# A graph network's attention sums: edges sorted within and across partitions, and bf16 one-hot products in place of f32 ones

## The chip, the cores and the metric

The kernel runs on one core of one Trainium2 chip. The metric is the device time of one execution in microseconds. The time before is the median of three runs. The profile is of one further execution, and all lengths inside the kernel come from it.

## The reference, cut to what matters

The input is 6250 nodes of 256 values and two edge lists. Four layers follow each other, each added to x: a graph convolution over 106,250 edges with 256 attributes each, an expert layer whose gates come from graph attention over 131,072 other edges, a second graph convolution, and a second expert layer. The change concerns the attention (`x` is the normalised node matrix, `M` the number of nodes):

```python
h = (x_flat @ W_gat).reshape(M, HEADS, NUM_EXPERTS)          # 4 heads, 4 experts
a_src = (h * att_src).sum(-1); a_dst = (h * att_dst).sum(-1)
e = leaky_relu(a_src[src] + a_dst[dst], 0.2)
ee = exp(e - segment_max(e, dst)[dst])
denom = segment_sum(ee, dst)
msg = h[src] * (ee / (denom[dst] + 1e-16))[:, :, None]
agg = segment_sum(msg, dst) + b_gat       # then a norm, a mean over heads, the two best experts
```

Indices reach up to 8191 while there are 6250 nodes, and a source beyond the end counts as the last node: 23,793 edges come from the last node, 76,190 from the others, and the rest, whose destination lies outside, is dropped. The sum over edges with the same destination is what both versions do with matrix products.

## The kernel before, in words

Nodes lie in 49 blocks of 128, one node a partition. Three stages follow a short start.

**First layer** (to about 1263 us). A loop over 147 steps `q` (L1600) loads edge attributes, turns them on VectorE (`turn`, L1465), multiplies them in f32 (`hidden`, L1473, tile `ph`), adds gathered rows (`join`, L1483) and sums by destination (`add_up`, L1490, tile `pe`). The order of every engine is written by hand and pinned. In between, `steps(sort)` takes one or two steps of `sorting()` (L1582): the attention's edges are sorted here, ahead of their use. Each of the 128 partitions holds 1024 edges as one key each (`make_keys`, L1244: destination reversed, source in the low 13 bits, read as an f32). `sort_steps` (L1276) takes the eight largest of each partition (`V.max`) and strikes them out (`V.match_replace`), 106 times. `sorted_edges` (L1285) then takes the keys apart in one go: `src2` (source), `high` (destination's block), `low` (node in the block), the latter also turned and written to `low_dram`; it ends with 160 small memsets and a count of the edges that lie in their expected blocks.

**Attention and first expert layer** (about 1291 to 2345 us). After the sort a column holds one edge of each partition, and eight columns make a group `g`; there are 80 groups. Since each partition was sorted alone, the 128 edges of a column spread over up to 12 blocks; `near_blocks` (L932) states which. The loop at L2187 works on several groups at once, one round per group:

- `fetch` (L1772): eight indirect DMAs on GpSimd gather the source rows into `sg` (five buffers).
- `score` (L1777): `rb`, the group's `low` values broadcast from `low_dram`, becomes a one-hot tile in bf16 (L1785); products with `part`, the three bf16 parts of `a_dst`, give `pa` (L1789). `A` marks each edge's block.
- `weigh` (L1803): picks the block (`za`), sums (`z`), leaky relu, exp on ScalarE.
- `spread_out` (L1817): the payload, 20 values an edge, goes to a PSUM tile `px` (L1824); `pp` (L1831) is the payload laid out over all blocks of the group, f32; `B` (L1840) is the one-hot of `low`, f32.
- `add_up` (L1845): one f32 product per column, `po` += `B`.T `pp` (L1852), over all blocks at once; then `po` is added to `acc` (L1858).
- `count_last` (L1861): counts the edges from the last node by destination, in the first rounds.

Between these calls stand `slot()` calls (L2166), five in a round up to round 61 and four after it. Each advances the expert layer `experts1` (L1652) by one of its 396 steps (eight f32 records on TensorE; products `ph` with gelu on ScalarE into `hh`, and `py` into `ys`), and takes up the work that follows the gates (`gates`, `node_values`). Each engine works its instructions in order, nearly the order of these calls. A block's gates can start when no later group can add to it (`complete`).

**Second graph convolution and second expert layer** (2345 us to the end). Gathers on GpSimd (`hg`, L1128), one-hot tiles on VectorE and products `pe` on TensorE. It starts when the last node's `hp` is written. The flag `redo` runs a general path if a count says that an edge was missed.

Of the kernel before, what the change touches and what calls it, by code (L numbers as in the profile page):

```python
# [8 lines left out]
F32 = mybir.dt.float32  # L9
# [7 lines left out]
P = 128  # L17
# [10 lines left out]
class Ordered:  # L28
# [6 lines left out]
    def pin(self):  # L35

        new = []
        for i in reversed(self.traced):
            if i is self.at:
                break  # L40
            new.append(i)
        for i in reversed(new):
            if i.engine in self.last:
                self.tc.add_manual_dep(
                    i, self.last[i.engine],
                    mybir.DependencyInfo(
                        mybir.DependencyClass.NoSync, mybir.DependencyReason.DATA
                    ),
                    reason="keep_in_program_order",
                )  # L50
            self.last[i.engine] = i.name
        self.at = self.traced[-1]

# [815 lines left out]
def kernel(ctx: ExitStack, tc: tile.TileContext, a: dict, out: bass.AP):  # L869
# [49 lines left out]


    KA, KB, KT, KM, NK = 640, 544, 848, 596.0, 12
# [3 lines left out]
    assert C2 % 8 == 0 and KA % P == 0 and P % G == 0 and N <= 8192 - P and T >= NK  # L925
# [5 lines left out]

    def near_blocks(g):  # L932

        k = g * G + G / 2
        mid = k * (N / KM) / P
        spread_of = (C2 * (k / C2) * (1 - k / C2)) ** 0.5 * (N / KM) / P
        n = min(NK, int(-(-2 * (4.2 * spread_of + 0.9) // 1)))
        b0 = min(max(round(mid - n / 2), 0), T - 2)
        return b0, min(max(round(mid - n / 2) + n, b0 + 2), T) - b0
# [4 lines left out]
    with ExitStack() as fast:  # L944
# [12 lines left out]
        lane16 = const.tile([P, P], BF16, name="lane16")  # L957
        with tc.tile_pool(name="numbers", bufs=1) as numbers:
# [6 lines left out]
            V.tensor_copy(lane16, jn)  # L965
# [240 lines left out]

        def equal(pool, w, q):


            eq = pool.tile([P, G1 * P], F32, name="eq", bufs=3)  # L1210
# [28 lines left out]
        src2 = gat.tile([P, KA], I32, name="src2")  # L1239
        low = gat.tile([P, KT], BF16, name="low")  # L1240
        high = gat.tile([P, KT], BF16, name="high")
        good3 = gat.tile([P, 2, 2], F32, name="good3")

        def make_keys(ix, k):  # L1244
# [4 lines left out]
            for i in range(2):  # L1249
# [22 lines left out]
                raw[1], raw[1], 13, 0x10000000, op0=OP.logical_shift_left, op1=OP.bitwise_or  # L1272
# [3 lines left out]
        def sort_steps(k):  # L1276

            top = order[:, k * 8 : (k + 1) * 8]
            V.max(out=top, in_=key)
            yield  # L1280
            if k * 8 + 8 < KT:
                V.match_replace(out=key, in_to_replace=top, in_values=key, imm_value=0.0)
            yield

        def sorted_edges(pst, wk):  # L1285

            k = order.bitcast(I32)
            V.tensor_scalar(src2, k[:, 0:KA], 8191, None, op0=OP.bitwise_and)
            some = key[:, 0:KT]
            for v, s in ((high, 20), (low, 13)):  # L1290
# [4 lines left out]
                V.tensor_copy(some, vi)  # L1295
                V.tensor_scalar(some, some, -1.0, 127.0, op0=OP.mult, op1=OP.add)
                V.tensor_copy(v, some)
            for c in range(KA // P):
                pt = pst.tile([P, 4, P], F32, name="pt")
                TE.transpose(pt[:, 0, :], some[:, c * P : (c + 1) * P], ident)  # L1300
                lt = wk.tile([P, P], BF16, name="lt")
                SC.activation(lt, pt[:, 0, :], AF.Copy)
                SC.dma_start(low_dram[c * P : (c + 1) * P, :], lt)
            V.tensor_add(good2[:, 1:2], good3[:, 0, 0:1], good3[:, 1, 0:1])
            V.tensor_add(good2[:, 3:4], good3[:, 0, 1:2], good3[:, 1, 1:2])

            lim = key[:, 0:KA]
            for g in range(KA // G):
                V.memset(lim[:, g * G : (g + 1) * G], float(near_blocks(g)[0]))
            hit = order[:, 0:KA]  # L1310
            V.tensor_tensor(hit, high[:, 0:KA], lim, op=OP.is_ge)
            for g in range(KA // G):
                V.memset(lim[:, g * G : (g + 1) * G], sum(near_blocks(g)) - 0.5)
            V.tensor_tensor(lim, lim, high[:, 0:KA], op=OP.is_ge)
            V.tensor_mul(hit, hit, lim)
            V.tensor_reduce(good2[:, 0:1], hit, axis=AX.X, op=OP.add)
# [5 lines left out]
        with ExitStack() as layer:  # L1322
# [3 lines left out]
            order = srt.tile([P, KT], F32, name="order")  # L1326
# [109 lines left out]
            HS = D + 8  # L1436
            with (
# [144 lines left out]
                def sorting():  # L1582

                    for k in range(KT // 8):
                        yield from sort_steps(k)
                    sorted_edges(psm, wk)
# [49 lines left out]
        acc = sums.tile([P, T, HV], F32, name="acc")  # L1636
# [101 lines left out]
        with (  # L1738
# [6 lines left out]
            tc.tile_pool(name="px3", bufs=1, space=PSUM) as psx,  # L1745
# [9 lines left out]
            px = psx.tile([P, P + 2 * G * HV], F32, name="px")  # L1755
            lanes = px[:, 0:P]
            V.tensor_copy(lanes, lane)
# [3 lines left out]
            NA = KA // G  # L1761
            HG = G // 2
            rows, near, got, pas, zs, pps, Bs, pos = {}, {}, {}, {}, {}, {}, {}, {}
# [8 lines left out]
            def fetch(g):  # L1772
                got[g] = wk.tile([P, G, GW], F32, name="sg", bufs=5)
                for j in range(G):
                    gather(got[g][:, j, :], gat_dram, src2[:, g * G + j : g * G + j + 1])

            def score(g, half):  # L1777

                b0, n = near_blocks(g)
                if half == 0:  # L1780
# [4 lines left out]
                    V.tensor_scalar(rows[g], rows[g], pid, None, op0=OP.is_equal)  # L1785
                    pas[g] = psa.tile([P, G, NK * H], F32, name="pa")
                for j in range(half * HG, (half + 1) * HG):
# [6 lines left out]
                if half == 1:  # L1794
                    rows.pop(g)
                    near[g] = wk.tile([P, G, NK], F32, name="A", bufs=3)
                    V.tensor_tensor(
                        near[g][:, :, 0:n], lanes[:, None, b0 : b0 + n].to_broadcast([P, G, n]),
                        high[:, g * G : (g + 1) * G].unsqueeze(2).to_broadcast([P, G, n]),
# [3 lines left out]
            def weigh(g):  # L1803
                n = near_blocks(g)[1]
                za = wk.tile([P, G, NK, H], F32, name="za", bufs=1)[:, :, 0:n, :]
                V.tensor_mul(
                    za, pas.pop(g)[:, :, 0 : n * H].rearrange("p g (b h) -> p g b h", h=H),
                    near[g][:, :, 0:n].unsqueeze(3).to_broadcast([P, G, n, H]),
                )
                z = wk.tile([P, G, H], F32, name="z")  # L1810
                V.tensor_reduce(z, za.rearrange("p g b h -> p g h b"), axis=AX.X, op=OP.add)
                V.tensor_add(z, z, got[g][:, :, HV:])
# [4 lines left out]
            def spread_out(g, half):  # L1817


                n = near_blocks(g)[1]  # L1820
                at = P + g % 2 * G * HV
                pay = px[:, at : at + G * HV].rearrange("p (g v) -> p g v", v=HV)
                if half == 0:
                    V.tensor_mul(  # L1824
                        pay.rearrange("p g (x h) -> p g x h", h=H),
                        got.pop(g)[:, :, 0:HV].rearrange("p g (x h) -> p g x h", h=H),
                        zs.pop(g).unsqueeze(2).to_broadcast([P, G, X + 1, H]),
                    )
                js = slice(half * HG, (half + 1) * HG)
                pps[g, half] = wk.tile([P, HG, NK, HV], F32, name="pp", bufs=3)  # L1830
                V.tensor_tensor(  # L1831
                    pps[g, half][:, :, 0:n, :],
                    pay[:, js, :].unsqueeze(2).to_broadcast([P, HG, n, HV]),
                    near[g][:, js, 0:n].unsqueeze(3).to_broadcast([P, HG, n, HV]), op=OP.mult,
                )
                if half == 1:
                    near.pop(g)
                Bs[g, half] = wk.tile([P, HG, P], F32, name="B", bufs=3)
                k = g * G + half * HG
                V.tensor_tensor(  # L1840
                    Bs[g, half], lanes[:, None, :].to_broadcast([P, HG, P]),
                    low[:, k : k + HG].unsqueeze(2).to_broadcast([P, HG, P]), op=OP.is_equal,
                )

            def add_up(g, half):  # L1845
                b0, n = near_blocks(g)
                if half == 0:
                    pos[g] = pso.tile([P, NK, HV], F32, name="po")
                po = pos[g][:, 0:n, :]
                B, pp = Bs.pop((g, half)), pps.pop((g, half))  # L1850
                for j in range(HG):
                    TE.matmul(  # L1852
                        po.rearrange("p b v -> p (b v)"), B[:, j, :],
                        pp[:, j, 0:n, :].rearrange("p b v -> p (b v)"),
                        start=half == 0 and j == 0, stop=half == 1 and j == HG - 1,
                    )
                if half == 1:
                    V.tensor_add(acc[:, b0 : b0 + n, :], acc[:, b0 : b0 + n, :], po)  # L1858
                    pos.pop(g)

            def count_last(k):  # L1861

                b = wk.tile([P, G, P], BF16, name="b", bufs=1)
                V.tensor_tensor(
                    b, lanes[:, None, :].to_broadcast([P, G, P]),
                    low[:, k : k + G].unsqueeze(2).to_broadcast([P, G, P]), op=OP.is_equal,
                )
                q = wk.tile([P, G, T], BF16, name="q", bufs=1)
                V.tensor_tensor(
                    q, lane64[:, None, :].to_broadcast([P, G, T]),  # L1870
                    high[:, k : k + G].unsqueeze(2).to_broadcast([P, G, T]), op=OP.is_equal,
                )
                pc = psy.tile([P, 2, D], F32, name="py")[:, 0, :]
                for j in range(G):
# [752 lines left out]
```

## Time and profile before

| | |
|---|---|
| median of 3 runs | 4173.14 us (4166.47 to 4188.83) |
| the profiled execution's own time | 3417.51 us |
| its span, first to last instruction | 3415.6 us |
| TensorE clock granted, mean | 0.905 of full speed |
| busy: TensorE, VectorE, GpSimd, ScalarE | 3169.8, 2303.3, 2243.9, 1127.5 us |
| start; first layer; attention with expert layer; its tail; second half | 150; 1113 (and 28 of passage); 977; 77; 1071 us |

The first two rows differ by 22%: the profiled execution was quicker than the three timed ones. In the views below, a group is written as line, engine, operation, result <- operands, shapes and count, then its busy time and the mean of one in ns, then the idle time of the engine just before it and what ended that. An f32 product shows as two records. In a table of stretches each engine's busy time is followed by its number of instructions.

### The profile page before, as it was taken

The numbers are of one execution on the slowest core, as the hardware profiler recorded it, in microseconds if no ns is written. First come the engines' busy times: TensorE is split into PE (matmuls) and PEld (weight loads), VectorE is DVE, ScalarE is ACT, GpSimd is POOL, SyncE is SP. The second block draws the span as 40 slices with busy tenths as digits, with TensorE's granted clock in tenths as the row PEclk, the third lists the DMA queues.
The fourth block names the chain that finished last, engine by engine and source line by source line (L and its number), as shares of the span: only waits on it lengthen the run. The fifth ranks groups of instructions, "written<-read, shape, count | busy, mean of one in ns | idle before, by whom it ended". The sixth has DMA issues, their size and how long they took to land.

```text
span 3415.6 us, 57212 instructions
## 1 busy us (share of the span) xinstructions
PE 3169.8 (93%) x18509; PEld 2532.5 (74%) x18509; DVE 2303.3 (67%) x5687; ACT 1127.5 (33%) x2014; POOL 2243.9 (66%) x2364
## 2 busy tenths in 40 slices
PE   7899999999999989999999999995688988989998
PEld 5677777777777778888888888883456666666677
DVE  7788898888888867877575858775234444445464
ACT  4122222222222234445545455661012212212134
POOL 0677777677777746766555556625777777777773
PEclk9999999999999999999999999996567677677797
DMA  6899999999999953434343434443112222222221
GB/s 182 197 205 203 203 205 202 194 203 205 205 209 206 207 133 107 98 83 138 83 125 97 132 85 126 114 98 88 53 53 59 60 59 60 59 59 66 59 63 37
DMA packets 699200, 428.56 MB, mean 125 GB/s; under 512 B 531304, under 2 KB 640347, under 8 KB 698892
## 3 DMA queue, kind: packets, MB, share of 16 engines
q0 software_dynamic: 89408, 178.08, 23.1%
q1 hardware_dynamic: 366236, 187.21, 21.2%
q10 hardware_dynamic: 243248, 59.52, 9.9%
q8 instruction: 150, 2.46, 0.3%
q14 instruction: 158, 1.29, 0.1%
HBM read 382.05 MB, written 42.49 MB: 124 GB/s over the span
## 4 chain that ended last, share of the span: by engine, by line
PE 62%; POOL 12%; DMA 10%; issue 7%; DVE 5%; SPq 1%; ACT 1%; ACTq 0%; DVEq 0%; POOLq 0%
PE ph L1115 31%; POOL hg L1128 12%; PE py L1115 11%; PE po L1852 6%; PE pe L1509 5%; DMA hg<-hp_dram,src 5%; PE pt L1115 4%; DMA ea<-in_edge_attr_dram 3%; PE pe L2492 3%; DMA rb<-low_dram 1%; PE pa L1789 1%; PE pt L1109 1%; DVE et L1468 1%; DVE x_all L2033 1%; SPq L1146 0%
## 5 line engine op out<-in xcount | busy, mean ns | idle before, releaser
L1128 POOL DMA_INDIRECT h<-y_dram,src x882 | 840.6, 953 | 414.2 <-issue 261.4
L1128 POOL DMA_INDIRECT hg<-hp_dram,src x831 | 786.0, 946 | 267.9 <-issue 225.5
L1128 POOL DMA_INDIRECT sg<-gat_dram,src x640 | 612.4, 957 | 351.1 <-issue 161.6
L1115 PE MATMUL ph<-w1b,et 128*128 128x256 f32 x3528 | 825.9, 386 | 9.8 <-DVE et L1468 9.8
L1115 PEld LDWEIGHTS ph<-w1b,et 128*128 128x128 f32 x3528 | 657.3, 191 | 152.9 <-issue 70.5
L2492 PE MATMUL pe<-eq,hg 128*128 128x96 f32 (+15 forms) x2036 | 438.1, 352 | 151.1 <-DMA hg<-hp_dram,src 123.4
L2492 PEld LDWEIGHTS pe<-eq,hg 128*128 128x128 f32 x2036 | 385.7, 258 | 256.1 <-issue 94.1
L2471 DVE TENSOR_SCALAR eq<-px,dst,ew 128x96 f32<-128x96 f32 x831 | 262.0, 370 | 219.1 <-PE pe L2492 135.3
L1487 ACT ACTIVATE h<-h 128x1536 f32<-128x1536 f32 x147 | 218.2, 1484 | 552.4 <-DMA ea<-in_edge_attr_dram 206.5
L1115 PE MATMUL py<-w,hh 128*128 128x256 f32 x1568 | 383.8, 385 | 4.8 <-ACT hh L1688 4.3
L1115 PE MATMUL ph<-b_all,w 128*128 128x256 f32 (+1 forms) x1600 | 385.9, 380 | 0.8 <-ACT hh L1688 0.7
L1486 DVE TENSOR_TENSOR h<-ph,h 128x1536 f32<-128x1536 f32 x147 | 258.2, 1757 | 122.5 <-PE ph L1115 118.9
L1115 PEld LDWEIGHTS py<-w,hh 128*128 128x128 f32 x1568 | 289.1, 191 | 40.9 <-ACT hh L1688 6.5
L1115 PEld LDWEIGHTS ph<-b_all,w 128*128 128x128 f32 x1600 | 289.9, 190 | 32.9 <-ACT hh L1688 1.1
L1468 DVE STREAM_TRANSPOSE et<-ea 128x1536 f32<-128x1536 f32 x147 | 259.9, 1768 | 12.6 <-DMA ea<-in_edge_attr_dram 9.2
L1688 ACT ACTIVATE hh<-ph,b 128x256 f32<-128x256 f32 (+1 forms) x400 | 166.5, 467 | 278.9 <-PE ph L1115 277.9
L1852 PE MATMUL po<-pp,B 128*128 128x240 f32 (+10 forms) x1280 | 252.1, 337 | 2.3 <-DVE acc L1858 2.2
L1852 PEld LDWEIGHTS po<-pp,B 128*128 128x128 f32 x1280 | 215.6, 190 | 14.4 <-DVE acc L1858 2.9
L1509 PE MATMUL pe<-h,eq 128*32 128x257 f32 x3168 | 217.9, 385 | 0.0
L1509 PEld LDWEIGHTS pe<-h,eq 128*32 128x32 f32 x3168 | 96.3, 109 | 84.6 <-issue 31.9
L1831 DVE TENSOR_TENSOR pp<-px,A 128x960 f32<-128x960 f32 (+10 forms) x160 | 156.1, 975 | 3.8 <-PE po L1852 3.6
L1688 ACT ACT_TABLE_LOAD x98 | 125.7, 1283 | 53.9 <-PE ph L1115 48.3
(338 smaller groups left out, 3950.2 us busy)
## 6 DMA issues: line engine op xcount, KB each, us to landing
ea<-in_edge_attr_dram ACTq DMA_DIRECT2D x588, 96.0 KB
ea<-in_edge_attr_dram SPq DMA_DIRECT2D x588, 96.0 KB
y<-y SPq DMA_DIRECT2D x196, 128.0 KB
w<-in_L_ffn_W_dram SPq DMA_DIRECT2D x48, 512.0 KB
y<-ys SPq DMA_DIRECT2D x96, 256.0 KB
rb<-low_dram SPq DMA_DIRECT2D x80, 256.0 KB
h<-y_dram,src POOLq DMA_INDIRECT x882
hg<-hp_dram,src POOLq DMA_INDIRECT x831
```

Of the source, the lines that this page charges most:

```text
L1109: TE.transpose(pt[:, c, :], src[:, c * P : (c + 1) * P], ident)
L1115: TE.matmul(dst, lhs(c), rhs(c), start=c == 0, stop=c == n - 1)
L1128: GP.indirect_dma_start(out=dst, out_offset=None, in_=table[0:NP, :], in_offset=IndirectOffsetOnAxis(ap=idx, axis=0),)
L1468: V.transpose(et[q].rearrange("p c m k -> p m c k"), ahead.pop(q).rearrange("p i m (c k) -> p (i m) c k", c=2),)
L1486: V.tensor_add(h, ph.pop(q), h)
L1487: SC.activation(h, h, AF.Relu)
L1509: TE.matmul(sums[w][b * Q : (b + 1) * Q, :], eq[k][:, j, at], h[:, i * NT + j, 0:WS], start=g == 0 and j == NT - 1, stop=g == last_of[b] a ...
L1688: SC.activation(hidden[u][:, f, :n, :], ph[:, f - f0, :n, :], AF.Gelu, bias=b1[:, e, f : f + 1],)
L1831: V.tensor_tensor(pps[g, half][:, :, 0:n, :], pay[:, js, :].unsqueeze(2).to_broadcast([P, HG, n, HV]), near[g][:, js, 0:n].unsqueeze(3).to ...
L1852: TE.matmul(po.rearrange("p b v -> p (b v)"), B[:, j, :], pp[:, j, 0:n, :].rearrange("p b v -> p (b v)"), start=half == 0 and j == 0, stop ...
L2471: V.tensor_scalar(equals[k][:, j, :], lanes[:, 0:NW], dst_of[:, t : t + 1], ew[:, t : t + 1], op0=OP.is_equal, op1=OP.mult,)
L2492: TE.matmul(sums[b][:, lo - t0 * P : hi - t0 * P], hg[:, j, :], eq[:, j, lo - n0 : hi - n0], start=False, stop=after >= (t0 + n) * P,)
```

## The change

The sort becomes two sorting networks of max and min on VectorE. The first sorts each partition's 1024 keys down to runs of eight; TensorE turns the tile so that eight columns of 128 partitions lie in one row (`turn_keys`); the second network sorts those; a second turn puts them back. So a column now holds 128 edges with neighbouring destinations. `sorted_tiles` computes beforehand, from binomial means and deviations, which blocks each tile (column) can meet: one to seven, where the whole group met up to 12. There are 84 groups and 612 tiles. The counts are now a column of ones in the payload.

The payload is weighted in SBUF (`weight`) and split into three bf16 parts, by copies on ScalarE and subtractions on VectorE, 61 columns with the column of ones. `spread_out` makes one tile `E` per column: the one-hot over all nodes of the tile's blocks, in bf16, by one tensor_scalar. `add_up` makes one bf16 product per tile and block. Only `acc` at the end (in `gates`) adds the three parts up. `px`, `pp` and `B` go, `sg` has four buffers, `po` two PSUM banks. The buffers of `y` for even nodes lie in `gtab`. The core of the diff:

```diff
-            top = order[:, k * 8 : (k + 1) * 8]
-            V.max(out=top, in_=key)
-            if k * 8 + 8 < KT:
-                V.match_replace(out=key, in_to_replace=top, in_values=key, imm_value=0.0)
+        def sort_steps(here, there, least):
+            size = 2
+            while size <= C2:
+                step = size // 2
+                while step >= (least if size == C2 else 1):
...
+                    for some, up in runs if size < C2 else [(slice(0, 1), 0)]:
+                        x, y = a[:, some, :, 0, :], a[:, some, :, 1, :]
+                        V.tensor_tensor(b[:, some, :, up, :], x, y, op=OP.max)
+                        V.tensor_tensor(b[:, some, :, 1 - up, :], x, y, op=OP.min)
+                        yield
...
+        def turn_keys(pst, here, there):
+            for k in range(0, G, 4):
+                pt = pst.tile([P, 4, P], F32, name="pt")
+                for i in range(4):
+                    TE.transpose(pt[:, i, :], here[:, :, k + i], ident)
+                SC.activation(there[:, k : k + 4, :], pt, AF.Copy)
+                yield
+        def sort_all(pst):
+            yield from sort_steps(key, order, G)
+            yield from turn_keys(...)
+            yield from sort_steps(order, key, P)
+            yield from turn_keys(...)
...
-            lim = key[:, 0:KA]
-            for g in range(KA // G):
-                V.memset(lim[:, g * G : (g + 1) * G], float(near_blocks(g)[0]))
...
+        block = gat.tile([P, KA], BF16, name="block")
+        GP.memset(block, 0.0)
+        # ... 379 more memsets: each tile's first block
...
-                got[g] = wk.tile([P, G, GW], F32, name="sg", bufs=5)
+                got[g] = wk.tile([P, G, GW], F32, name="sg", bufs=4)
...
-                    pps[g, half][:, :, 0:n, :],
-                    pay[:, js, :].unsqueeze(2).to_broadcast([P, HG, n, HV]),
-                    near[g][:, js, 0:n].unsqueeze(3).to_broadcast([P, HG, n, HV]), op=OP.mult,
-                )
...
-                    Bs[g, half], lanes[:, None, :].to_broadcast([P, HG, P]),
-                    low[:, k : k + HG].unsqueeze(2).to_broadcast([P, HG, P]), op=OP.is_equal,
+            def weight(g, step):
+                m = len(tiles2[g])
+                parts = [pays[g % 2][:, 0:m, i * HV : (i + 1) * HV] for i in range(3)]
+                if step == 0:
+                    pay[g] = wk.tile([P, G, HV], F32, name="pay", bufs=1)[:, 0:m, :]
+                    V.tensor_mul(pay[g]..., got.pop(g)..., zs.pop(g)...)
+                    SC.activation(parts[0], pay[g], AF.Copy)
+                elif step == 1:
+                    V.tensor_sub(pay[g], pay[g], parts[0])
+                    SC.activation(parts[1], pay[g], AF.Copy)
+                else:
+                    V.tensor_sub(parts[2], pay.pop(g), parts[1])
+            def spread_out(g, j):
...
+                Es[g, j] = wk.tile([P, NM, P], BF16, name="E", bufs=EB)
+                V.tensor_scalar(
+                    Es[g, j][:, 0:n, :].rearrange("p b k -> p (b k)"), nodes16[:, 0 : n * P],
+                    bits.bitcast(F32)[:, g * G + j : g * G + j + 1], None, op0=OP.is_equal,
+                )
...
-                    TE.matmul(
-                        po.rearrange("p b v -> p (b v)"), B[:, j, :],
-                        pp[:, j, 0:n, :].rearrange("p b v -> p (b v)"),
+                for b in range(b0, b0 + n):
+                    bank, to = divmod(b - u0, UB)
+                    TE.matmul(
+                        pos[g][:, bank, to * HP : (to + 1) * HP], E[:, b - b0, :],
+                        pays[g % 2][:, j, :], start=bank not in begun,
...
+                def spread_and_sum(i):
+                    for q in (2 * i, 2 * i + 1):
+                        if there in range(NA):
+                            spread_out(there, q)
+                        g, j = divmod(there * G + q - LAG, G)
+                        if g in range(NA):
+                            add_up(g, j)
```

Here `EB` is 6 and `LAG` 4: the product of a tile is issued four tiles after its `E`. In a round the calls stand in the order `weight(there, 1)`, `spread_and_sum(0)`, slot, `score(now, 0)`, slot, `weight(there, 2)`, `spread_and_sum(1)`, `weigh(here)`, slot, `spread_and_sum(2)`, slot, `score(now, 1)`, slot, `weight(here, 0)`, `spread_and_sum(3)`, `count_last`.

## The prediction

> **What bounds the kernel now.** I first cut the span into stages (busy time of each engine in six stretches; TensorE, its weight loads, VectorE, ScalarE, GpSimd, granted clock, DMA share, GB/s).
>
> ```profile
> 150.00:1263.00 1113.00, 1091.34 (x7233) 845.18 (x7232) 948.51 (x1645) 309.93 (x522) 803.84 (x844) 1.00 0.99 201
> 1291.00:2268.00 977.00, 966.34 (x6696) 857.35 (x6695) 706.66 (x1723) 490.11 (x856) 612.40 (x640) 1.00 0.41 108
> 2268.00:2345.00 77.00, 54.29 (x310) 43.70 (x310) 61.20 (x203) 37.91 (x79) 15.44 (x15) 0.85 0.38 113
> 2345.00:3416.00 1071.00, 916.76 (x3604) 677.02 (x3603) 468.10 (x1763) 225.67 (x416) 774.60 (x820) 0.72 0.20 57
> ```
>
> The second row is the attention stage with the expert layers, 80 rounds at 12.2 us. TensorE is busy 99% of it; VectorE has 270 us to spare. The change sits here, and its sort in the first row, also TensorE's. The last row it does not touch. A busy sum can hide waits, so I read next the groups of the attention stage:
>
> ```profile
> L1852 PE MATMUL po<-pp,B 128*128 128x240 f32 (+10 forms) x1208 | 242.6, 341 | 2.3 <-DVE acc L1858 2.2
> L1831 DVE TENSOR_TENSOR pp<-px,A 128x960 f32<-128x960 f32 (+9 forms) x154 | 153.4, 996 | 3.8 <-PE po L1852 3.6
> L1840 DVE TENSOR_TENSOR B<-px,low 128x512 f32<-128x512 f32 x154 | 105.0, 682 | 0.0
> L1785 DVE TENSOR_SCALAR rb<-rb,pid 128x1024 bf16<-128x1024 bf16 x80 | 39.7, 496 | 58.3 <-DMA rb<-low_dram 57.9
> L1858 DVE TENSOR_TENSOR acc<-acc,po 128x240 f32<-128x240 f32 (+8 forms) x75 | 27.4, 365 | 122.1 <-PE po L1852 122.1
> ```
>
> TensorE hardly waits before `po`, while VectorE waits 122 us for `po` before it can add it to `acc`: TensorE sets the pace. What a matmul really takes is the distance of starts, since the listed durations overlap (timeline of TensorE):
>
> ```profile
> 1702.59 1.78 PE L1852 MATMUL po<-pp,B 128*128 128x240 f32 x8
> 1704.21 1.89 PE L1115 MATMUL ph<-b_all,w 128*128 128x256 f32 x8
> 1705.94 0.46 PE L1789 MATMUL pa<-part,rb 128*128 128x48 bf16 x12
> 1706.24 1.97 PE L1115 MATMUL py<-w,hh 128*128 128x256 f32 x8
> 1708.05 1.78 PE L1852 MATMUL po<-pp,B 128*128 128x240 f32 x8
> ```
>
> Four f32 `po` (8 records) take 1.62 us, 0.202 a record; one step of the expert layers takes 1.73; a bf16 `pa` takes 0.30/12 = 0.025; the layer step behind `pa` takes 1.81, so going back to f32 costs 0.08. GpSimd has a fixed beat, here in the first layer and the same in all stages:
>
> ```profile
> 103.06 0.95 POOL L1128 DMA_INDIRECT h<-y_dram,src  x1 [0.30 <-issue]
> 104.31 0.95 POOL L1128 DMA_INDIRECT h<-y_dram,src  x1 [0.30 <-issue]
> ```
>
> A gather every 1.25 us: eight take 10.0 us of the 12.2 us round.
>
> **What the Trainium skill says.** "TensorE: Matmul & The Clock Gate", section "Wait — 56ns, not 53.3ns?": starts are never closer than about 25 ns, however few columns. The 25 ns of `pa` agree. "VectorE: DVE Perf Modes", section "The perf-mode tier table (the rule you actually need)": tensor_scalar on bf16 in SBUF runs at the fourfold rate, an f32 tensor_tensor at the single. The trace agrees: `rb` takes 496 ns for 1024 columns (486 is the median), `pp` about 1 ns a column. "SBUF — State Buffer", section "Who interferes with whom": VectorE in a two-port mode and GpSimd shut each other out. The trace shows a little: 29 gathers that ran beside `rb` lasted 1.01 us on average, the others 0.95.
>
> **The change, part by part.** Replaying the new schedule gives 84 rounds for 80, 612 tiles for 640, and 2116 products of one tile with one block; sorting the given edges the new way puts all of them inside the tiles' blocks.
>
> *TensorE in the rounds.* Out go 1280 `po` records of 198 columns on average: 0.84 ns a column (0.202/240), so 213 us. In come 2116 bf16 products of 61 columns; the trace has 48 columns at 25 ns, I take 28: 59 us (25 and 50 ns as ends: 53 to 106). They are cut in four pieces a round, each followed by f32 work: 4 x 84 x 0.08 = 27 us. `pa` and counting lose 84 and 89 small products, -4 us. Four more rounds carry 11 more steps of the expert layers, +19 us, which the tail then lacks. Sum: -112 us, 977 to 865.
>
> *VectorE in the rounds.* Out: `pp` and `B`, -258 us. In: 612 `E`, a fixed 206 ns (a 128x1 tensor_scalar with a pointer, `off` L2321) and 280 ns per 1024 columns (486 less 206): 612 x 0.206 + 2116 x 0.035 = 200 us. Two subtractions a round at 0.33 us (as `px`, L1824): +55. `acc` now adds 61 columns for each of 865 blocks in 145 pieces: 145 x 0.19 + 53 = 81 for 27, +54. Narrower `za` and `z` -15, counting -3. Net +33, but listed times overlap by some 0.06 us each (their sum was 810 in these rounds for 707 busy), and 620 more instructions take 37 of it back: VectorE stays at 700 us, 8.3 a round, hidden under TensorE's 10.3 but closer than before. If `E` ran at the single rate (1 ns a column), it would be 900, 10.7 a round.
>
> *ScalarE* gets two copies a round, 168 x 0.28 = 47 us on 490, under cover. *GpSimd*: 612 x 1.25 = 765 us; if each `E` held one gather up by 0.06 us, 802. Its buffers go from 5 to 4, but are freed about as early (end of round k-1). It bounds a round at 10.0, close to TensorE's 10.3: what is late next, if TensorE gets quicker still, is the gather. SP has 4 more `rb` loads and the same `y` traffic; even nodes' `y` go into `gtab`, free since round 1: nothing.
>
> Waits: TensorE lost some 25 us in 977. With three engines within 20% I allow 30 more (ends: 0 and 110). Rounds: 977 - 112 + 30 = 895. **-82**.
>
> *Tail* (2268 to 2345): 11 layer steps fewer, 19 us; the gates of the last five nodes come four rounds later as before. **-14** (-25 to 0).
>
> *First layer.* The old sort ends in one block of VectorE work (timeline near its end):
>
> ```profile
> 1218.44 0.33 PE L1300 MATMUL pt<-ident,key 128*128 128x128 f32 x1 [3.63 <-DVE key L1296]
> 1232.90 0.94 POOL L1128 DMA_INDIRECT h<-y_dram,src  x1 [11.81 <-issue]
> ```
>
> TensorE waits for `key`, then until 1230.3 for VectorE, and GpSimd stands for 12 us: about 11 us are lost. The new one yields between pieces and has no 160 memsets: -11. It has 202 steps for some 223 places, so it ends inside the layer. 380 max/min at about 0.41 us (a 256-column tensor_tensor) are 160 us for 251, hidden as before under TensorE. New on TensorE: 16 transposes at 0.11, and waits for VectorE before each batch: +4 (0 to 15). The 380 GpSimd memsets (0.12 us for the 128x1 in the trace: 47 us) end before the first gather at 101.65, nothing; over 0.26 each they would delay it. **-7**.
>
> Sum: -103 on the profiled execution's 3417.5 (span 3415.6 and 1.9 around it): 3314. The median of the runs shown is 4173, 22% above, and no view shows why. If the extra is a constant, the gain stays 103 (4070); if TensorE was slower in those runs, by 756 us over its 2060 in the first two stages, a factor of 1.37, it is about 170 (4003): TensorE's terms grow, and the added waits vanish as the others get slack. In proportion it is 126. I take 133: **4040**.
>
> **The rivals.** *As worked out* (0.64): 3975 to 4090. *Lockstep eats most of it* (0.20): VectorE and GpSimd each have under two us of slack a round, `E` has six buffers and is used four tiles later, so every stall spreads. At 11.2 us a round, 84 make 941: -57 with tail and first layer, 4100 to 4165. For it: the 58 us that VectorE already waits for `rb`; against: TensorE's four pieces a round give half a round of lead.
>
> *Slower* (0.14): VectorE waits on ScalarE. `pay` is split as copy, subtract, copy, subtract across the two engines, in order on each. Each copy stands behind a gelu that waits for `ph` and perhaps behind a table load (1.28 us). Behind the waiting subtraction stand the `E` of the next tiles, which TensorE waits for. Two waits of 1.7 us, 1.6 for `acc`, on 8.3: 13.3 us a round, 1117 in all, +140 in the rounds, about 4290. It decides from 11.6 us of VectorE per round, waits included (977/84). Against it: each copy has two `E` and a piece of a round between it and its reader.
>
> *The change doesn't do what it says* (0.02): a miscount runs the general path too, far above any range; the replay speaks against it.
>
> **How the numbers follow.** A measurement can tell about 0.5%, 21 us, from no change. Faster: the first case and most of the second, 0.79; same 0.06; slower 0.15. The range goes from the first case at the factor 1.37 with no added waits (about 3960) up to 4190, which takes in the second case and the start of the third.
>
> **What would show it.** Right: `po` starts 28 ns apart; rounds (`rb` to `rb`) near 10.5 us; VectorE near 700 us with waits for `po`; no stop at the sort's end; last stage unchanged. Wrong: `E` above 480 ns on average; subtractions with idle before them put down to ScalarE; gathers well above 0.95 us; TensorE waiting for `E`.

## The result, and the profile after

| | kernel before | changed kernel | ratio (95%) |
|---|---|---|---|
| median of 20 runs each | 4191.05 us (4164.90 to 4215.82) | 4216.61 us (4193.39 to 4243.34) | 1.0066 (1.0047 to 1.0086) |
| the same two kernels in a later set, 15 and 4 runs | 3426.93 us | 3346.09 us | 0.9769 (0.9749 to 0.9789) |

The change costs 0.7% where it was forecast to gain 3%. Every set of runs is made on one chip, and in each set all executions of the kernel before lay at one of two levels, 3417 to 3435 us or 4165 to 4306 us; I call them the 3425 level and the 4200 level. The level doesn't go with the chip's number: the record gives number 5 for a set at 3427 us and for one at 4184 us some twenty minutes later. The profile of before that the prediction was made from is of the 3425 level, the three timed runs beside it and the twenty of the result are of the 4200 level. At the 3425 level the change gains 2.3%; before that set ran, 0.968 to 0.982 had been expected at this level if the prediction's steps hold there, and 0.995 to 1.01 if they hold nowhere.

The page of the changed kernel at the 4200 level (the share of the span that each engine is busy; then the head of the chain of work that ended last):

```profile
span 4204.6 us, 59695 instructions
PE 3228.3 (77%) x19189; PEld 2462.9 (59%) x19189; DVE 2163.3 (51%) x6247; ACT 1191.3 (28%) x2207; POOL 2250.8 (54%) x2720
PE 32%; another core or an unknown queue 11%; issue 7%; DVE 6%; POOL 3%; ACT 3%; DMA 2%; SPq 0%; DVEq 0%; ACTq 0%; POOLq 0%
```

TensorE is busy 77% of the span where the first profile of before had 93%, and over the whole span no engine is near its limit. Of the chain 11% is put down to "another core or an unknown queue", though the kernel has one core only; the profile of before at this level has 17% of it, the two profiles at the 3425 level none. The 7% of "issue" stands in those as well and tells nothing. The stages (table of stretches, columns as in the prediction: TensorE, weight loads, VectorE, ScalarE, GpSimd, clock, DMA share, GB/s), first of the changed kernel at the 4200 level, then of before at that level, then of the changed kernel at the 3425 level; the second row of each is the rounds:

```profile
150.00:1525.00 1375.00, 1206.52 (x7385) 901.79 (x7385) 853.62 (x1565) 316.66 (x531) 825.66 (x852) 0.93 0.74 165
1561.00:2841.00 1280.00, 977.19 (x7514) 786.06 (x7515) 678.47 (x2382) 561.42 (x1048) 589.49 (x609) 0.89 0.33 83
2899.00:4205.00 1306.00, 891.27 (x3622) 662.02 (x3622) 469.94 (x1779) 223.43 (x416) 783.92 (x831) 0.71 0.18 47
```

```profile
150.00:1546.00 1396.00, 1185.54 (x7342) 880.82 (x7341) 964.75 (x1663) 314.26 (x526) 811.00 (x850) 0.93 0.71 162
1571.00:2862.00 1291.00, 1067.72 (x6695) 906.42 (x6694) 708.76 (x1720) 490.65 (x855) 612.41 (x640) 0.92 0.31 82
2924.00:4244.00 1320.00, 894.95 (x3622) 669.08 (x3622) 476.19 (x1789) 223.82 (x416) 787.82 (x831) 0.70 0.16 47
```

```profile
150.00:1278.00 1128.00, 1103.65 (x7261) 852.68 (x7260) 839.30 (x1538) 312.72 (x526) 812.76 (x844) 0.99 0.96 199
1315.00:2195.00 880.00, 854.25 (x7516) 726.47 (x7516) 672.98 (x2383) 559.33 (x1048) 602.22 (x609) 0.99 0.45 121
2254.00:3343.00 1089.00, 920.63 (x3622) 678.12 (x3622) 469.64 (x1777) 225.66 (x416) 783.98 (x831) 0.72 0.20 57
```

Read down one column at a time. The work of three engines in a stage hardly depends on the level (rounds of the changed kernel: VectorE 678 and 673, ScalarE 561 and 559, GpSimd 589 and 602), but the length does: 1280 us against 880. At the 4200 level every stage is longer, also those that the change does not touch. At the 3425 level the rounds take 880 us with the change and 977 without it. At the 4200 level they take 1280 and 1291, but from two sets whose medians of before differ by 1.5% (4191 and 4256 us): brought to the first set in proportion, the 1291 are about 1271 (an estimate), so nothing of the gain is left.

TensorE's busy time does grow (977 against 854), and its granted clock is lower (0.89 against 0.99; before: 0.92 against 1.00). The clock alone doesn't explain the length: the rounds of before at 0.92 would take some 1062 us (an estimate, 977/0.92), not 1291. Whether the lower clock comes of the stops shown next or has a cause of its own is not shown.

What fills the difference shows in the timeline of the changed kernel at the 4200 level, here in the first layer:

```profile
632.73 0.19 PEld L1160 LDWEIGHTS ph<-w1b,et 128*128 128x128 f32 x1 [1.02 <-issue]
632.85 3.39 ACTq L1477 DMA_DIRECT2D ea<-in_edge_attr_dram  x4
633.45 0.38 PE L1160 MATMUL ph<-w1b,et 128*128 128x256 f32 x1 [1.06 <-issue]
634.16 0.19 PEld L1160 LDWEIGHTS ph<-w1b,et 128*128 128x128 f32 x1 [1.25 <-issue]
635.56 0.38 PE L1160 MATMUL ph<-w1b,et 128*128 128x256 f32 x1 [1.74 <-issue]
636.27 0.29 PEld L1160 LDWEIGHTS ph<-w1b,et 128*128 128x128 f32 x1 [1.93 <-issue]
636.98 0.59 PE L1160 MATMUL ph<-w1b,et 128*128 128x256 f32 x1 [1.04 <-issue]
638.39 0.50 PEld L1160 LDWEIGHTS ph<-w1b,et 128*128 128x128 f32 x2 [1.83 <-issue]
```

The starts of matmuls and weight loads, taken together, lie 0.71 us apart, or twice that (633.45, 634.16, 635.56, 636.27, 636.98, 638.39), where an f32 matmul otherwise follows the last every 0.22 us, and nothing is waited for ("issue"). Distances of 0.69 to 0.73 us occur some 200 times in this trace and 9 times in the first profile of before; SyncE's records show the same beat (247 times against 18). All of TensorE's distances over 0.6 us sum to 1206 us, against 412 in the changed kernel at the 3425 level: these 794 us are most of the 861 by which the two spans differ. Before has 1118 us at the 4200 level and 358 at the other.

### The profile page after: what moved, and what is told of

It is laid out like the page before. It is cut to its first block, busy times and chain, and to the rows that moved or that the text cites. A ratio compares the mean times of both kernels' runs of the same rounds, so it can differ in the third digit from the quotient of the medians.

```text
span 4204.6 us, 59695 instructions
## 1 busy us (share of the span) xinstructions
PE 3228.3 (77%) x19189; PEld 2462.9 (59%) x19189; DVE 2163.3 (51%) x6247; ACT 1191.3 (28%) x2207; POOL 2250.8 (54%) x2720
## 4 chain that ended last, share of the span: by engine, by line
PE 32%; another core or an unknown queue 11%; issue 7%; DVE 6%; POOL 3%; ACT 3%; DMA 2%; SPq 0%; DVEq 0%; ACTq 0%; POOLq 0%
PE ph L1160 11%; PE py L1160 11%; PE pe L2658 4%; POOL hg L1173 2%; PE pt L1160 2%; PE po L1982 1%; DMA rb<-low_dram 1%; PE pa L1907 1%; DVE E L1962 1%; DVE eq L2637 1%; DVE acc L1993 0%; DVE x_all L2613 0%; DVE x_all L2181 0%; POOL sg L1173 0%
## 5 line engine op out<-in xcount | busy, mean ns | idle before, releaser
L1160 PE MATMUL ph<-w1b,et 128*128 128x256 f32 x3528 | 868.8, 399 | 35.5 <-issue 25.5
L1160 PEld LDWEIGHTS ph<-w1b,et 128*128 128x128 f32 x3528 | 683.3, 199 | 202.9 <-issue 111.1
L1160 PE MATMUL py<-w,hh 128*128 128x256 f32 x1568 | 442.8, 421 | 63.8 <-ACT hh L1787 27.9
L2658 PE MATMUL pe<-eq,hg 128*128 128x96 f32 (+15 forms) x2036 | 373.7, 333 | 145.3 <-issue 64.4
L1160 PE MATMUL ph<-b_all,w 128*128 128x256 f32 (+1 forms) x1600 | 453.6, 421 | 12.4 <-issue 12.2
L1586 DVE TENSOR_TENSOR h<-ph,h 128x1536 f32<-128x1536 f32 x147 | 258.2, 1757 | 373.7 <-remote 156.7
L1609 PE MATMUL pe<-h,eq 128*32 128x257 f32 x3168 | 258.0, 402 | 54.1 <-issue 51.9
L1962 DVE TENSOR_SCALAR E<-nodes,bits 128x256 bf16<-128x256 bf16 (+5 forms) x612 | 186.4, 340 | 208.0 <-remote 83.3
L1160 PE MATMUL py<-ew,g 65*128 65x256 f32 x392 | 137.4, 475 | 44.6 <-DVE x_all L2613 21.4
L1982 PE MATMUL po<-pays,E 128*128 128x61 bf16 x2116 | 113.4, 197 | 75.8 <-DVE acc L1993 34.8
L1160 PE MATMUL ph<-b_all,ew 128*128 128x512 f32 (+2 forms) x256 | 121.3, 602 | 59.1 <-ACT g L2573 33.3
```

The source lines that it names most:

```text
L1160: TE.matmul(dst, lhs(c), rhs(c), start=c == 0, stop=c == n - 1)
L1586: V.tensor_add(h, ph.pop(q), h)
L1609: TE.matmul(sums[w][b * Q : (b + 1) * Q, :], eq[k][:, j, at], h[:, i * NT + j, 0:WS], start=g == 0 and j == NT - 1, stop=g == last_of[b] a ...
L1962: V.tensor_scalar(Es[g, j][:, 0:n, :].rearrange("p b k -> p (b k)"), nodes16[:, 0 : n * P], bits.bitcast(F32)[:, g * G + j : g * G + j + 1 ...
L1982: TE.matmul(pos[g][:, bank, to * HP : (to + 1) * HP], E[:, b - b0, :], pays[g % 2][:, j, :], start=bank not in begun, stop=bank not in lat ...
L2658: TE.matmul(sums[b][:, lo - t0 * P : hi - t0 * P], hg[:, j, :], eq[:, j, lo - n0 : hi - n0], start=False, stop=after >= (t0 + n) * P,)
```

## The experiments

Theory A: at the 4200 level the time follows the number of instructions, not TensorE's time; the change adds 2483. Theory F: both count. Others are named where they are stated. All ratios are to the kernel before of the same set.

**Before once more.** No edit.

> The kernel before, unchanged, profiled once more. Its first profile is of an execution of 3417 us, while its timed runs took 4165 to 4216. If this execution is like the timed runs (4160 to 4220), its profile is the one to set beside the one of after (4206). Theory A (a hindrance that the first profile did not have is in both kernels): first layer about 1500 us in place of 1256, attention rounds about 1280 us in place of 977, TensorE busy only three quarters of the span, the same stops of TensorE with multiples of 0.70 us between instructions. Theory B (after has brought the stops): this profile has TensorE busy in nine tenths, and its gaps over 0.6 us sum to some 360 us as in the first one.

4245.57 us; its stages are shown above. Theory B falls: the stops are in both kernels (1118 us in this one), and the first profile of before was no measure of the runs at the 4200 level.

**The new sort alone**, with its tiles (`eq4` and the key buffers), in the kernel before:

```diff
-                    for k in range(KT // 8):
-                        yield from sort_steps(k)
+                    yield from sort_all(psm)
```

> The kernel before with the new sort only (two networks of max and min, turns on TensorE); the count of edges in their blocks and its 160 small memsets stay, and the attention stage is that of before. Theory A (time follows instructions and stops, not TensorE's products): about as before, ratio 1.000 to 1.005, since the sort issues some 200 instructions more. Theory C (the sort's 380 steps of VectorE lengthen the first layer by as much as attention gains): ratio 1.010 to 1.020, first layer 40 to 80 us longer. My prediction's step: 7 us less, ratio 0.998.

0.9984 (0.9960 to 1.0007), 4200 level. The sort is not what costs; theory C falls.

**Instructions that nobody waits for**, in the rounds of before:

```diff
+            def extra(n):
+                for _ in range(n):
+                    V.memset(spare, 0.0)
...
                 slot()
+                extra(6)
```

> The kernel before with about 2600 memsets of 128x1 on VectorE scattered over the attention rounds, which nobody waits for: about as many further instructions as the change brings (2483), some 150 us of VectorE, which had 270 us of slack in these rounds in the first profile. Theory A (in ordinary runs the time follows the number of instructions): at 4190 us for 57212 instructions it would be 73 ns each, 190 us more, ratio 1.045; at the least 13 ns each, 35 us, ratio 1.008. Theory D (instructions cost only their own engine's time, and VectorE has room): ratio within 1.003.

> The 2600 memsets of 128x1 on VectorE in the rounds once more. On a chip where before takes 3420 us: theory H (what an instruction costs there is only its engine's time, VectorE has room): within 1.004; theory F2 (an added instruction costs 35 to 40 ns on any chip): ratio 1.025 to 1.03. On a chip where before takes 4200 us: 1.02 to 1.03 as in the first run.

At the 4200 level 1.0227 (1.0154 to 1.0300), at the 3425 level 1.0001 (0.9991 to 1.0012). The rounds at either level:

```profile
1585.00:2963.00 1378.00, 1096.86 (x6674) 925.08 (x6673) 797.06 (x4185) 498.62 (x862) 611.00 (x640) 0.90 0.29 76
1296.00:2268.00 972.00, 962.96 (x6679) 857.44 (x6678) 795.19 (x4185) 498.59 (x862) 609.90 (x640) 1.00 0.41 108
```

VectorE does the same work in both, 797 and 795 us. In the second row it is busy 82% and the rounds are no longer than without the memsets (977); in the first it is busy 58% and they are 87 us longer (1291 in the same set). So at the 4200 level 2559 more instructions cost 97 us (0.0227 of 4256; the interval, from four runs, reaches from 66 to 128), 38 ns each, though their engine is idle 42% of the time.

**TensorE's time without its instructions.** Seven of eight products `po` of a group take one block's columns only:

```diff
+                    m = n if half == 0 and j == 0 else 1
-                        pp[:, j, 0:n, :].rearrange("p b v -> p (b v)"),
+                        pp[:, j, 0:m, :].rearrange("p b v -> p (b v)"),
```

> The kernel before with its 640 f32 products po left at the same number, but seven of the eight of a group multiply the columns of one block only (20 instead of up to 240); the other blocks' sums are left out. TensorE's own time falls by about 168 us (7/8 of 213, times 178/198), no instruction is added or removed. Theory A (the ordinary rounds follow the number of instructions alone): ratio 0.995 to 1.003. Theory F (TensorE's time and the number of instructions both count; the change's gain on TensorE was real and was paid back by its 2500 instructions): rounds 80 to 170 us shorter, ratio 0.96 to 0.98.

> The products po over one block (the other blocks' sums are left out), number of instructions unchanged, for a chip where before takes about 4200 us. Theory A (there the time follows the number of instructions, not TensorE's time): ratio 0.996 to 1.002. Theory F (both count): 70 to 90 us less as on the quicker chip, ratio 0.978 to 0.985. Where before takes 3420 us: 0.977 as three times before.

At the 3425 level 0.9778 (0.9761 to 0.9795), and 0.9765 and 0.9771 in two repetitions; at the 4200 level 1.0034 (1.0010 to 1.0058). The rounds at the 3425 level, then at the 4200 level:

```profile
1298.00:2195.00 897.00, 894.40 (x6696) 795.98 (x6695) 696.97 (x1722) 502.09 (x865) 616.27 (x640) 1.00 0.45 117
1558.00:2842.00 1284.00, 1038.00 (x6692) 873.10 (x6691) 693.74 (x1720) 501.44 (x864) 613.65 (x640) 0.87 0.31 82
```

This is what decides: the same cut shortens the rounds from 977 to 897 us at one level, and doesn't shorten them at the other (1284; before has 1291 in a set whose median is 1.7% longer). The whole kernel is 0.3% slower there, just above theory A's range and far from F's. What this cut takes off TensorE is worth nothing at the 4200 level, and theory F falls for it. At the 3425 level TensorE's time counts, as F says, but the number of instructions doesn't (the memsets: 1.0001). The 168 us that I had written down for the cut were too many (last section).

**One part of the payload in place of three**, in the changed kernel: no copies, no subtractions, products of 21 columns.

> The changed kernel with the payload rounded to one bf16 part; the two further parts are left out: no copies on ScalarE, no subtractions on VectorE, products of 21 columns in place of 61, acc a third as wide. Theory E (the handover between VectorE and ScalarE and the wider sums in acc eat the gain): 60 to 130 us faster than after, ratio to before 0.975 to 0.99. Theory A (time follows instructions): 504 instructions fewer of 59695, at 13 to 73 ns each 7 to 37 us faster than after, ratio to before 0.998 to 1.005.

0.9989 (0.9967 to 1.0010) at the 4200 level, so 0.8% or 32 us below the changed kernel, whose 439 further instructions would then cost 74 ns each. It lies in A's range and outside E's; but the price is twice that of the memsets, so the number of instructions isn't the whole of it. The 32 us compare two sets, each through its own kernel before.

**Fewer instructions on TensorE**, in the changed kernel: the three bf16 parts of `a_dst` side by side, one product `pa` per tile in place of three; `za` and its sum are three times as wide. Nothing is left out. The edit also gives `pa` one PSUM buffer in place of two and calls `weigh` one slot earlier.

```diff
-                    for i in range(3):
-                        TE.matmul(pas[g][:, j, 0 : n * H], rows[g][:, j, :],
-                            part[:, i, b0 : b0 + n, :]..., start=i == 0, stop=i == 2)
+                    TE.matmul(pas[g][:, half, at : at + n * 3 * H], rows[g][:, j, :],
+                        part[:, b0 : b0 + n]..., start=True, stop=True)
```

> The changed kernel with one product pa per tile over the three parts of a_dst side by side, in place of three: 1224 products and 1224 weight loads fewer on TensorE (30 us of its time), za and its sum three times as wide and in two pieces, 168 instructions and some 40 us more on VectorE; nothing is left out. Where before takes about 4200 us: theory A1 (40 ns for each instruction on any engine) 90 us less than after, ratio to before 0.98 to 0.99; theory A2 (only the instructions of VectorE and ScalarE count there, at 40 to 70 ns) 5 to 15 us more than after, ratio 1.007 to 1.012. Where before takes 3420 us, TensorE's 30 us against VectorE's 40: ratio 0.968 to 0.98, beside 0.977 for after.

> The changed kernel with one product pa per tile over the three parts of a_dst, once more: 57415 instructions in place of 59695. Where before takes about 4200 us: theory A1 (40 ns for each instruction on any engine) ratio to before 0.98 to 0.99; theory A2 (only the instructions of VectorE and ScalarE count there) 1.007 to 1.012. Where before takes 3420 us: 0.972 as in the run before.

0.9723 (0.9694 to 0.9753) at the 3425 level, 0.9925 (0.9885 to 0.9965) at the 4200 level: faster than before at either level. It is faster than the changed kernel too, clearly at the 4200 level; at the 3425 level by 0.5%, with intervals that just meet (0.9749). The rounds at the 4200 level:

```profile
1573.00:2803.00 1230.00, 942.27 (x6290) 752.92 (x6290) 764.35 (x2531) 550.29 (x1040) 587.92 (x609) 0.89 0.32 87
```

Against the changed kernel VectorE has 86 us more to do and the rounds are 50 us shorter. 2235 instructions fewer bring 59 us (1.0066 less 0.9925, of 4190; the two intervals allow about 40 to 80), 26 ns each: A1's direction, two thirds of its size; A2 (only VectorE's and ScalarE's instructions count) falls. What the earlier `weigh` and the one buffer do was not tried apart.

**The new tiles with f32 sums** (`pp`, `B` and `po` as before, but each product only over its own tile's blocks, and one opening product on zeros a group; 144 instructions more than before).

> The new sort, tiles and groups of the changed kernel with the sums of the kernel before: pp and B in f32 as before, one f32 product po per tile, but only over the blocks of that tile (612 products of 73 columns on average in place of 640 of 198); counts by a column of ones. No E, no parts, no subtractions. About 57300 instructions, as the kernel before; TensorE some 125 us less, VectorE some 100 us less in the rounds. Theory F: 80 to 130 us faster, ratio 0.97 to 0.98, quicker than both kernels. Theory A: ratio 0.995 to 1.003.

0.9947 (0.9929 to 0.9964), twice more 0.9935 and 0.9936, all at the 3425 level; not seen at the other. A miss: I expected 80 to 130 us and got 20. Its rounds are only 33 us shorter (944), as `po` shrinks to 0.110 us a record and no further, and as one early round takes 49 us beside gathers that run back to back (the first eight rounds take 117 us, 98 in the changed kernel).

**Small instructions elsewhere**, in before: 1695 copies on ScalarE in the rounds; memsets beside the last stage's one-hot tiles, three and then two each.

> The kernel before with about 1700 copies of one column on ScalarE scattered over the attention rounds, which nobody waits for: 340 us of ScalarE, which is busy 490 of some 1290 us there. Theory A and F (an added instruction costs 35 to 40 ns in ordinary runs, on whatever engine): 60 to 70 us more, ratio 1.014 to 1.017. Theory D2 (the 2600 memsets cost 106 us because VectorE is on the path in the rounds, not because they were instructions): within 1.004, since ScalarE stays below 70%.

> The kernel before with three memsets of 128x1 on VectorE after each one-hot tile of the second graph convolution: 2493 more instructions, in a stage in which VectorE is busy a third of the time and GpSimd's gathers set the pace. Theory A and F (35 to 40 ns for each instruction, in any stage): 87 to 100 us more, ratio 1.021 to 1.024. Theory D2 (VectorE's own place in the rounds): within 1.004. If an added instruction costs something only where the stage has many: ratio 1.005 to 1.015.

> The kernel before with two memsets of 128x1 on VectorE after each one-hot tile of the second graph convolution, 1662 instructions more, none of them after the last tile. Where before takes about 4200 us: theories A and F (an instruction costs 40 ns there, in any stage) 66 us more, ratio 1.016; theory D2 (the memsets in the rounds cost time because VectorE is on the path there) within 1.004. Where before takes 3420 us: within 1.002.

All three met the 3425 level and so say nothing on theory A, nor on D2: that the memsets in the rounds cost 97 us at the 4200 level because VectorE is on the path there, and not as instructions, is not excluded. Against it stands that VectorE is busy 58% of those rounds, and that fewer instructions on TensorE gained. The copies cost 1.66% (1.0148 to 1.0185), 57 us. 31 of them show as a wait: TensorE's products `py` waited 35.0 us for ScalarE's `hh`, 4.3 us before. ScalarE's slack of half a round is no slack for the product that stands behind it. The three memsets cost 2.28% by a fault of the experiment: some 700 of them stood behind the last gather, where the end of the kernel grew from 47 to 130 us; the 1750 or so within the last stage left it at 1036 us (before 1038). With two each the ratio was 1.0022 (1.0013 to 1.0031), and the end again grew, to 58 us.

## Why the prediction was wrong, and where it was right

**At the level of its profile it was right in mechanism and near in size.** Forecast: 103 us less; measured: 81 by the medians, 72 by the spans of the two profiles, which come from different sets. Step by step at the 3425 level:

- *TensorE in the rounds*: forecast -112 us; measured 966 to 854 busy, -112. That the sum meets to the microsecond is partly luck, as its smaller terms were not measured one by one. The large one was: in the timeline nine products `po` take 0.26 us, from 1800.23 to 1800.49, 29 ns each (forecast 28), some 61 us for 2116 of them:

```profile
1800.23 0.42 PE L1982 MATMUL po<-pays,E 128*128 128x61 bf16 x9
1800.49 1.97 PE L1160 MATMUL ph<-b_all,w 128*128 128x256 f32 x8
1802.30 0.27 PE L2222 MATMUL py<-ident,b_all 128*128 128x128 f32 x1
```

- *VectorE*: forecast 700, measured 673. *The waits*: forecast +30; TensorE is not busy for 26 us in 880 where it was for 11 in 977, +15. The groups within the rounds:

```profile
L1962 DVE TENSOR_SCALAR E<-nodes,bits 128x256 bf16<-128x256 bf16 (+5 forms) x612 | 185.4, 346 | 56.7 <-PE po L1982 56.0
L1982 PE MATMUL po<-pays,E 128*128 128x61 bf16 x2104 | 101.4, 192 | 9.0 <-DVE acc L1993 9.0
L1993 DVE TENSOR_TENSOR acc<-acc,po 128x488 f32<-128x488 f32 (+7 forms) x140 | 69.7, 532 | 0.8 <-PE po L1982 0.7
L1954 DVE TENSOR_TENSOR pays<-pay,pays 128x160 bf16<-128x160 f32 (+3 forms) x80 | 24.9, 312 | 12.4 <-ACT pays L1952 12.2
```

`E` takes 346 ns on average (forecast 327; the single rate would have been above 480). TensorE waits 9 us for `acc` and does not wait for `E`. The subtraction that is shown waits 12 us for ScalarE in all rounds together and the other one 3, not 3 us in each round: the rival that ends on the slower side, VectorE waiting on ScalarE's copies, did not happen. Lockstep, at 941 us for the rounds, didn't either.
- *Rounds*: forecast 977 to 895, measured 880, 10.5 us each. *Gathers*: 989 ns each in these rounds, 957 before; inside the bounds. Those that ran beside an `E` took no longer than the others (989 and 988 ns). That eight of them bound a round at 10.0 us was too high: 612 in 84 rounds are 7.3 a round, 9.1 us.
- *Last stage and tail*: forecast 0 and -14. With the border at the first gather `hg` (2330 us before, 2254 after) the last stage takes 1086 and 1089 us and the tail 62 and 59, -3.
- *First layer*: forecast -7, measured +24 (first round at 1315 for 1291). Three things were missed. The stage lies near GpSimd's bound too: 882 gathers at the beat of 1.25 us are 1102 of the 1154 us between the first and the last, and a gather now takes 964 ns on average for 953. The stop of the gathers at the sort's end did not go (11.8 us before; 6.2 and 2.7 after). The last gather comes 10.5 us later, part of which is scatter: in three other traces at this level that have the first layer of before it comes 3 to 7 us later too. And the diff gives the last node's `eq` one buffer (`eq4`) where it had three. VectorE before (two rows), then after:

```profile
1255.51 1.01 DVE L1217 TENSOR_TENSOR eq<-lane,dst 128x384 f32<-128x384 f32 x2
1260.55 1.02 DVE L1217 TENSOR_TENSOR eq<-lane,dst 128x384 f32<-128x384 f32 x2
```

```profile
1274.41 1.03 DVE L1270 TENSOR_TENSOR eq<-lane,dst 128x384 f32<-128x384 f32 x2 [8.27 <-PE pe L1601]
1283.58 1.03 DVE L1270 TENSOR_TENSOR eq<-lane,dst 128x384 f32<-128x384 f32 x2 [6.47 <-PE pe L1601]
```

Each `eq` now waits for the products that read the one before it, and from the last gather to the first round it takes 49 us for 36, 13 more. That wait was written in the diff, and I passed over it as room made for the sort. It was not tried with the buffers given back; the new sort alone has the one buffer too, and its rounds begin 8 us later than those of before in its set.

**The step that failed** is the one from the profile to the median: "The median of the runs shown is 4173, 22% above, and no view shows why. If the extra is a constant, the gain stays 103 (4070); if TensorE was slower in those runs ... it is about 170 (4003) ... I take 133". All its cases had TensorE's time count in those runs, and none had a term for the number of instructions. TensorE's time does not count there (po cut short: 1.0034 against 0.9778), while added instructions cost time (memsets: 1.0227 against 1.0001) and fewer save it (merged products: 1.4% less than the change). The change takes 112 us off TensorE, which gains nothing at the 4200 level, and adds 2483 instructions. That these are what turned the gain into a loss of 0.7% fits in sign, but is argued from those two experiments and not shown by itself. The Trainium skill's "TensorE: Matmul & The Clock Gate" (section "Wait — 56ns, not 53.3ns?"), from which I took the floor between starts, agrees with the traces: in the changed kernel's profile at the 3425 level the starts of `pa` lie 25 ns apart (median) at every width from 4 to 28 columns, and those of `po`, 61 columns wide, 28. The price that decided is in no row of the first profile.

**What stays open.** Why there are two levels, and what the stops are. Transfers are no slower where they occur (queue q1 took 16.4% of 16 engines over 4244 us, 21.2% over 3416: less in all), nor is VectorE (its `h` takes 1757 ns at both), so it lies in the time around instructions, but no run takes that apart. The fetching of instructions, an obvious suspect, doesn't look different: the queue q8 moves 150 packets in both profiles of before, 1.08 and 1.05 us each (median), and the stops don't gather about them. The recording is another that no run tests: the record has a span and a granted clock for every execution, the timed ones too, so none shows the time without it. Nor does the account close: 2483 instructions at 26 to 38 ns are 65 to 94 us, and the change costs 28 (0.0066 of 4191). Where the rest went is not shown; the price differed between experiments (26, 38 and 74 ns), so it may depend on the instruction or on where it stands.

## What to carry to other kernels

Before a gain read from a profile is put on other executions, see whether these have its length; where they are a fifth longer with the same busy times, the profile's bound is not theirs, and a change should be costed in instructions as well as in time. A change that lowers both, such as three products laid side by side into one, was quicker than before at either level. And read the buffers in a diff as steps of their own: where one tile went from three buffers to one, 13 us were lost beside a stage that the change was not about.

## What the runs showed of the hardware that I had not expected

Narrow f32 products with 128 columns of weights stop getting quicker. In the first profile of before a `po` record of 240 columns starts 0.203 us after the last, one of 160 0.136 and one of 140 0.119 (medians), but those of 120, 100 and 60 columns all 0.112. Cut from 240 to 20 columns, the median is 0.112 and the mean 0.098; eight records (timeline of TensorE, po over one block) still take 0.81 us with the change to the next product:

```profile
1710.03 0.96 PE L1853 MATMUL po<-pp,B 128*128 128x20 f32 x8
1710.84 1.54 PE L1115 MATMUL ph<-b_all,w 128*128 128x256 f32 x6
```

So the cut saved some 70 to 80 us and not 168, all of which came off the rounds at the 3425 level; and narrowing f32 products (the new tiles with f32 sums) saves less than their columns say, while the bf16 products of the change go down to 0.028. What sets this limit was not tried. The other surprise is that one program had two speeds, 3425 and some 4200 us, with the same busy times of VectorE, ScalarE and GpSimd, and that a memset for which nobody waits was free at the first and cost 38 ns at the second.
